# Mamba layers in a four-layer kernel: the residual by TensorE, the softplus correction by ScalarE and GpSimd, the norm's affine part in the weights

## The chip, the cores and the metric

The kernel runs on one core of a Trainium2 chip. A core has five instruction streams: TensorE (PE, matrix products into PSUM), VectorE (DVE), ScalarE (ACT), GpSimd (POOL) and SyncE (SP), which here issues all DMA transfers. The streams run side by side and wait for each other by semaphores; each works through its own list in order. The metric is the time of one execution on the device in microseconds (us). Everything is float32.

## The reference

The input has 4 images of 96 channels and 64 x 64 points. Four layers follow each other: a Mamba layer, a state-space layer over four scan directions, a second Mamba layer and a ConvNeXt block. The change concerns the two Mamba layers only. Each treats an image as a sequence of L = 4096 tokens and runs two sublayers, then a 1x1 fusion and a batch norm. A sublayer is, cut to what matters:

```python
h = (seq - mu) * rsqrt(var + EPS) * ln_g + ln_b
xs, z = split(h @ in_w)                               # 192 + 192 channels
xc = silu(conv_b + sum(conv_w[:, k] * xp[:, k:k+L] for k in range(4)))   # xp: xs padded by 3
dt, Bm, Cm = split(xc @ xproj_w)                      # 6 + 16 + 16
delta = softplus(dt @ dt_w + dt_b)
# for each channel d and state s of 16, along the sequence:
#   state = exp(delta * A) * state + delta * Bm * xc
y = sum over s of state * Cm + Dp * xc
seq = seq + (y * silu(z)) @ out_w
```

The softplus of x is max(x, 0) + ln(1 + u), with u = exp(-|x|). Since u is small here and 1 + u is rounded, the kernel adds a correction: what was lost in the rounding, u - ((1 + u) - 1).

## The kernel before

One function, `mamba_fusion`, runs a Mamba layer. All four images stay in the tile `X` (96 channels on the partitions). Work goes in 32 steps: 2 pairs of images, times 2 sublayers, times 8 chunks of 512 tokens. A step has two parts.

The *front* (`mamba_front`, a generator) turns a chunk of both images of a pair into what the scans need. It normalises (`pc` and `pv` are matmuls for the centred values and the variance, L172 and L179; DVE multiplies, L184; POOL applies `ln_g` and `ln_b`, L185) into the tile `h`. A row of ones below the 96 channels serves for the convolution's bias. The convolution and the input projection are one set of matmuls, `pu` (L194), as are those for z, `pz` (L204). `pd` (L217) gives dt, B and C; `rows` and `bc` carry B and C through DRAM, to be spread over partitions. Then come three tiles of softplus (`pt` L235, function `softplus` L260 to L271), `du` = delta times xc (L248, POOL), and the stores of delta and du to DRAM (`dd` and `dg`, L251).

The *scan* (class `Scan`) treats a step as 24 groups of 2 x 512 columns on 128 partitions (8 channels by 16 states). A group needs exp(delta A) and delta B x. `load` brings delta from DRAM, spread over the states (`da`, L295); ACT takes the exponential (L107). For 18 of 24 groups the second term is a matmul that spreads `du` (`bs`, L313), multiplied by B on DVE (L335); for the other six ("dma" in the code) it is loaded and multiplied on POOL (L308). DVE runs two scans a group (`hs`, L340), POOL multiplies by C (`hc`, L342), and PE sums over the states (`py`, L361). After eight groups `close` (L369) multiplies by the gate, and for each image `project` (L377, into `po`) and a DVE addition to `X` (L381) end the sublayer. After the second sublayer, `fuse` applies the 1x1 fusion (`pf`, L510), takes the statistics (`bn_stats`, L512) and stores `X` to DRAM (`raw`, L513).

`Scan.run` writes the order. A slot is one group; stages run at a lag to it: loads 4 slots ahead, `spread` one ahead, `sums` two behind, `close` three, `project` four, `fuse` five behind. In each slot it also advances the front of the next step, as many pieces as the list `PACE` says:

```python
for lag, what in ((4, self.project), (5, self.fuse)):
    if (g := at(lag)) and g["last"] and g["j"] and (g["sub"] or lag == 4):
        what(g, g["j"] - 1)
for _ in range(PACE[slot] if slot < len(PACE) else 0):
    next(ahead, None)
```

The pieces with the softplus fall in the last slots of a step, beside the scans of groups 16 to 23 of the step before (counting groups from 0 in their step). From this program a scheduler derives the final order of each engine, and moves an instruction by some places. Buffers matter too: `bs` has two PSUM tiles[...], the front's matmuls share two banks under the tag `mm`, `py` and `po` (with `pf`) have one each; `hs` and `hc` have three buffers, `da` and `du` loads share six.

Of the kernel before, what the change touches and what calls it, by code (L numbers as in the profile page):

```python
# [18 lines left out]
F32 = mybir.dt.float32  # L19
AF = mybir.ActivationFunctionType  # L20
ALU = mybir.AluOpType
# [55 lines left out]
class Consts:  # L77
    def __init__(self, tc, pool):
        nc = tc.nc
        self.act = Tables(tc)  # L80
        self.norms = [pool.tile([C, 2], F32, name=f"bn{i}") for i in range(2)]
        self.ident = pool.tile([P, P], F32, name="ident")
        make_identity(nc, self.ident)

        self.center = pool.tile([C, C], F32, name="center")
        nc.vector.tensor_scalar(self.center, self.ident[:C, :C], -1.0 / C, None, ALU.add)
        self.mean = pool.tile([C, C], F32, name="mean")
        nc.vector.memset(self.mean, 1.0 / C)
        self.eps = pool.tile([P, 1], F32, name="eps")
        nc.vector.memset(self.eps, EPS)  # L90


class Tables:
# [61 lines left out]
def mamba_front(tc, k, X, pools, wt, pair, c, h, made):  # L155

    nc = tc.nc  # L160
    work, psum, dram = pools
    if c == 0:
        nc.vector.memset(h[:C, :, 0:3], 0.0)
    else:
        nc.scalar.copy(h[:C, :, 0:3], h[:C, :, T : T + 3])

    def bank(name):
        return psum.tile([P, T], F32, tag="mm", name=name)

    for b in range(2):  # L170
        pc = bank("pc")[:C]
        nc.tensor.matmul(  # L172
            pc, lhsT=k.center, rhs=X[:, 2 * pair + b, ds(c * T, T)], start=True, stop=True
        )
        sq = work.tile([P, T], F32, tag="ua", name="sq")[:C]
        nc.scalar.activation(sq, pc, AF.Square)
        yield
        pv = bank("pv")[:C]
        nc.tensor.matmul(pv, lhsT=k.mean, rhs=sq, start=True, stop=True)  # L179
        rs = work.tile([P, T], F32, tag="lg", name="rs")[:C]  # L180
        rsqrt(k.act, rs, pv, k.eps[:C])
        yield
        dst = h[:C, b, 3 : 3 + T]
        nc.vector.tensor_tensor(dst, pc, rs, ALU.mult)  # L184
        nc.gpsimd.tensor_scalar(dst, dst, wt["ln"][:, 0:1], wt["ln"][:, 1:2], ALU.mult, ALU.add)  # L185


    xz = made["xz"] = work.tile([P, 6, T], F32, name="xz", bufs=2)
    for j in range(3):
        pu = bank("pu")  # L190
        for tap in range(4):
            kk = C + 1 if tap == 3 else C
            for r0, r1, d0, d1, b in SEGS[j]:
                nc.tensor.matmul(  # L194
                    pu[r0:r1], lhsT=wt["conv"][:kk, tap, d0:d1], rhs=h[:kk, b, ds(tap, T)],
                    start=(tap == 0), stop=(tap == 3),
                )
            yield
        nc.scalar.copy(xz[:, j], pu)
    k.act.other(xz[:, :3], xz[:, :3], AF.Silu)  # L200
    for j in range(3):
        pz = bank("pz")
        for r0, r1, d0, d1, b in SEGS[j]:
            nc.tensor.matmul(  # L204
                pz[r0:r1], lhsT=wt["in"][:, DIN + d0 : DIN + d1], rhs=h[:C, b, 3 : 3 + T],
                start=True, stop=True,
            )
        yield
        nc.scalar.copy(xz[:, 3 + j], pz)


    dbl = work.tile([P, T], F32, name="dbl")
    pd = bank("pd")
    for n in range(2):
        for b in range(2):
            j, r0, r1 = ROWS[b][n if b == 0 else 1 - n]
            nc.tensor.matmul(  # L217
                pd[2 * QUART * b : 2 * QUART * (b + 1)], lhsT=wt["xproj"][r0:r1, j],
                rhs=xz[r0:r1, j], start=(n == 0), stop=(n == 1),
            )  # L220
    yield
    nc.scalar.activation(dbl, pd, AF.Identity, bias=wt["one"])


    rows = dram.tile([P, T], F32, name="rows")
    nc.sync.dma_start(rows, dbl)
    bc = made["bc"] = work.tile([P, 2, 2, T], F32, name="bc", bufs=2)


    du = made["du"] = work.tile([P, 3, T], F32, name="du", bufs=2)  # L230
    for j in range(3):
        pt = bank("pt")
        for r0, r1, d0, d1, b in SEGS[j]:
            half = ds(HALFP * b, HALFP)
            nc.tensor.matmul(  # L235
                pt[r0:r1], lhsT=wt["dt"][half, d0:d1], rhs=dbl[half], start=True, stop=True,
            )
        delta = work.tile([P, T], F32, name="delta", bufs=2)
        softplus(nc, k.act, work, delta, pt)
        yield  # L240
        if j == 0:
            for b in range(2):
                for q in range(2):
                    r = HALFP * b + (QUART if q else RANK + 1)
                    nc.sync.dma_start(
                        bc[:, b, q], rows[r : r + NST, None].to_broadcast([NST, HEIGHT, T])
                    )
        nc.gpsimd.tensor_tensor(du[:, j], delta, xz[:, j], ALU.mult)  # L248
        for name, x in (("dd", delta), ("dg", du[:, j])):
            made[name, j] = dram.tile([P, T], F32, name=f"{name}{j}")  # L250
            nc.sync.dma_start(made[name, j], x)  # L251
    k.act.other(xz[:, 3:], xz[:, 3:], AF.Silu)

PACE = (1,) * 8 + (2,) + (1,) * 7 + (2,) + (1,) * 7
LEAD = 4


def softplus(nc, act, work, out, x):  # L260

    u = work.tile([P, T], F32, tag="ua", name="ua")
    t = work.tile([P, T], F32, tag="lg", name="lg")
    nc.scalar.activation(u, x, AF.Abs)
    act.exp_ln(u, u, AF.Exp, scale=-1.0)
    act.exp_ln(t, u, AF.Ln, bias=1.0)
    nc.vector.scalar_tensor_tensor(out, x, 0.0, t, ALU.max, ALU.add)
    nc.scalar.activation(x, u, AF.Identity, bias=1.0)

    nc.vector.scalar_tensor_tensor(t, x, 1.0, u, ALU.subtract, ALU.subtract, reverse1=True)  # L270
    nc.gpsimd.tensor_tensor(out, out, t, ALU.add)  # L271


class Scan:
# [7 lines left out]


    def __init__(self, tc, k, X, pools, sel, carry, fuse):
        self.tc, self.k, self.X, self.sel, self.carry, self.fuse = tc, k, X, sel, carry, fuse
        self.state, self.psum = pools

    def load(self, g):
# [82 lines left out]
    def project(self, g, b):  # L371

        nc = self.tc.nc
        xz, wt = g["made"]["xz"], g["wt"]
        po = self.psum.tile([P, T], F32, tag="po", name="po", bufs=1)[:C]
        for n, (j, r0, r1) in enumerate(ROWS[b]):
            nc.tensor.matmul(  # L377
                po, lhsT=wt["out"][r0:r1, j], rhs=xz[r0:r1, j], start=(n == 0), stop=(n == 1)
            )
        xs = self.X[:, 2 * g["pair"] + b, ds(g["c"] * T, T)]  # L380
        nc.vector.tensor_tensor(xs, xs, po, ALU.add)  # L381

    def run(self, steps, wts, front, first):

# [9 lines left out]
        ]  # L394
        total, each = len(groups), len(units)
        ahead = iter(())
        for n in range(-4, total + 6):
            slot = (n + LEAD) % each
            if slot == 0:
                for _ in ahead:  # L400
# [4 lines left out]
            def at(lag):  # L405
                return groups[n - lag] if 0 <= n - lag < total else None
# [6 lines left out]
                if g := at(lag):  # L413
                    stage(g)

            for lag, what in ((4, self.project), (5, self.fuse)):
                if (g := at(lag)) and g["last"] and g["j"] and (g["sub"] or lag == 4):
                    what(g, g["j"] - 1)
            for _ in range(PACE[slot] if slot < len(PACE) else 0):
                next(ahead, None)  # L420


def mamba_weights(nc, act, ident, wpool, w, sub, one7):
    wt = {"one": one7}

    def load(name, shape):
        wt[name] = wpool.tile(shape, F32, name=f"w_{name}{sub}")
        nc.sync.dma_start(wt[name], w[name][sub])

    load("ln", [C, 2])  # L430
    load("in", [C, 2 * DIN])
    conv = wt["conv"] = wpool.tile([C + 1, 4, DIN], F32, name=f"w_conv{sub}")
    nc.sync.dma_start(conv[:C], w["conv_wT"][sub].partition_broadcast(C))
    nc.sync.dma_start(conv[C : C + 1, 3], w["conv_b"][sub : sub + 1])
    nc.vector.tensor_tensor(
        conv[:C], conv[:C], wt["in"][:, None, :DIN].to_broadcast([C, 4, DIN]), ALU.mult
    )
    xp = wt["xproj"] = wpool.tile([P, 3, 2 * QUART], F32, name=f"w_xproj{sub}")
    nc.vector.memset(xp, 0.0)
    nb = RANK + 1 + NST  # L440
# [26 lines left out]
def mamba_fusion(ctx: ExitStack, tc, k, src, dst, w):  # L467
# [38 lines left out]
    def fuse(g, b):  # L506
# [2 lines left out]
        pf = psum.tile([P, T], F32, tag="po", name="pf", bufs=1)[:C]  # L509
        nc.tensor.matmul(pf, lhsT=fus[:, 0], rhs=xs, start=True, stop=True)  # L510
        nc.scalar.activation(xs, pf, AF.Identity, bias=gb[:, b : b + 1])
        nc.vector.bn_stats(stats[:, b * NT + c], xs)  # L512
        nc.sync.dma_start(dst[b, :, ds(c * T, T)], xs)  # L513

    wts = [mamba_weights(nc, k.act, k.ident, one, w, 0, one7)]
    carry = one.tile([P, 3, P // HEIGHT], F32, name="carry")
    steps = [(pair, sub, c) for pair in range(B // 2) for sub in range(2) for c in range(NT)]

# [10 lines left out]
    for n, _ in enumerate(front(0, made)):  # L529
        if n % 4 == 3 and n // 4 - 1 in range(B):  # L530
            b = n // 4 - 1
            nc.vector.reduce_sum(gsum[:, b : b + 1], X[:, b], axis=AX.X)
    wts.append(mamba_weights(nc, k.act, k.ident, one, w, 1, one7))

    gpw = one.tile([C, C], F32, name="gpw")
    nc.sync.dma_start(gpw, w["gp_wT"])
# [12 lines left out]
    gb = one.tile([C, B], F32, name="gb")  # L549
    nc.scalar.activation(gb, pg2, AF.Identity, bias=vec[:, 1:2])  # L550

    Scan(tc, k, X, (state, psum), sel, carry, fuse).run(steps, wts, front, made)

    norm = k.norms.pop()
    mv = one.tile([C, 2], F32, name="mv")
# [733 lines left out]
```

## Time and profile before

| | |
|---|---|
| runs of the kernel before | 10000.75, 10018.09, 10055.14 us (median 10018.09) |
| profiled execution, its own time | 10010.64 us |
| its span, first to last instruction | 10008.9 us |
| busy, share of the span | PE 86%, DVE 82%, POOL 70%, ACT 55% |
| granted TensorE clock, mean | 0.939 of full speed |

"Busy" counts an engine's instructions, not its waits. The shares are means over four layers with different limits, so the stages are read apart. In a row of instruction groups, `L342 POOL TENSOR_TENSOR hc<-hs,bc 128x1024 x391` is line 342 on POOL, writing `hc` from `hs` and `bc` on 128 partitions by 1024 elements, 391 times; then busy time, the mean duration in ns, the engine's idle time just before these instructions, and what ended it. A float32 matmul counts as two instructions.

### The profile page before, as it was taken

To read this page: it belongs to the slowest core of one execution; us is meant where nothing else is said; L and a number is where in the kernel's file an instruction comes from. 1 tells how busy PE (TensorE), PEld (TensorE's weight loads), DVE (VectorE), ACT (ScalarE), POOL (GpSimd) and SP (SyncE) were. 2 spreads that over 40 slices of the span, in tenths; PEclk is the share of its full clock that TensorE was granted. 3 is DMA by queue.
4 is the path that set the end of the run, shared out by engine and by line. 5 is a ranking of instruction groups with operands and counts; after the bars stand their busy time and mean duration, and the time that the engine had idled before them with its cause. 6 is when DMAs were issued, how large, how long until landed. Compare 5 with 4: busy or idle time off the path is not lost. (4 is left out here: it accounts for less than half of the span.)

```text
span 10008.9 us, 110272 instructions
## 1 busy us (share of the span) xinstructions
PE 8562.4 (86%) x33120; PEld 3566.0 (36%) x33120; DVE 8200.6 (82%) x10877; ACT 5497.9 (55%) x10460; POOL 6966.5 (70%) x4600
## 2 busy tenths in 40 slices
PE   7888888888886888888888888788888888887688
PEld 1222212222214766666776676122222222221122
DVE  7999999999994666667666666799999999999787
ACT  5566666656653445445445444566666665665244
POOL 6888888888883555555555555688888888888322
PEclk9999999999997999999999999899999999999798
DMA  7777777777773223223222221777777767777442
GB/s 190 200 205 204 201 206 207 201 201 209 204 197 105 72 66 94 65 66 95 72 66 74 81 64 51 188 201 204 210 200 203 208 196 204 207 204 199 113 99 73
DMA packets 802257, 1527.53 MB, mean 153 GB/s; under 512 B 123933, under 2 KB 127161, under 8 KB 800890
## 3 DMA queue, kind: packets, MB, share of 16 engines
q1 hardware_dynamic: 801658, 1520.47, 54.6%
q8 instruction: 263, 4.31, 0.2%
q14 instruction: 336, 2.75, 0.1%
HBM read 1229.30 MB, written 155.98 MB: 138 GB/s over the span
## 5 line engine op out<-in xcount | busy, mean ns | idle before, releaser
L342 POOL TENSOR_TENSOR hc<-hs,bc 128x1024 f32<-128x1024 f32 x1536 | 3608.0, 2355 | 622.2 <-DVE hs L340 554.8
L340 DVE TENSOR_TENSOR_SCAN hs<-da,carry,bs 128x512 f32<-128x512 f32 x2016 | 2466.4, 1264 | 79.2 <-POOL du L308 1.0
L107 ACT ACTIVATE da<-da,w_a 128x512 f32<-128x512 f32 x2304 | 1616.5, 716 | 1268.5 <-DMA da<-dd 1218.7
L361 PE MATMUL py<-hc,selsum 128*32 128x512 f32 x6144 | 1801.4, 638 | 462.5 <-POOL hc L342 448.3
L313 PE MATMUL bs<-du,seldu 64*128 64x512 f32 x4608 | 1573.3, 676 | 204.2 <-DVE hs L340 194.5
L335 DVE TENSOR_TENSOR bs<-bs,bc 128x1024 f32<-128x1024 f32 x1152 | 1397.7, 1213 | 184.0 <-PE bs L313 181.6
L308 POOL TENSOR_TENSOR du<-du,bc 128x1024 f32<-128x1024 f32 x384 | 904.5, 2355 | 281.3 <-DMA du<-dg 160.5
L863 POOL TENSOR_TENSOR seg<-seg,cb 128x384 f32<-128x384 f32 x512 | 514.7, 1006 | 818.1 <-DVE cb L862 750.0
L361 PEld LDWEIGHTS py<-hc,selsum 128*32 128x32 f32 x6144 | 240.6, 110 | 1815.1 <-POOL hc L342 1118.2
L313 PEld LDWEIGHTS bs<-du,seldu 64*128 64x128 f32 x4608 | 446.0, 195 | 1196.2 <-DVE hs L340 852.1
L848 DVE TENSOR_SCALAR seg<-dr,dac 128x128 f32<-128x128 f32 x1536 | 660.4, 458 | 256.9 <-PE y L892 249.3
L194 PE MATMUL pu<-h,w_conv 96*128 96x512 f32 (+3 forms) x2048 | 834.6, 629 | 6.5 <-ACT rs L107 6.3
L340 DVE TENSOR_TENSOR_SCAN hs<-bs,carry,du 128x512 f32<-128x512 f32 x672 | 823.5, 1260 | 7.8 <-issue 5.0
L799 PE MATMUL front<-pk,sconv 128*128 128x512 f32 x1536 | 767.9, 609 | 9.2 <-ACT z L787 5.1
L915 ACT ACTIVATE y<-yz 128x192 f32<-128x192 f32 x512 | 186.0, 363 | 919.3 <-DVE yz L914 918.3
L867 POOL TENSOR_TENSOR xs<-pre,coef 128x576 f32<-128x576 f32 x512 | 598.3, 1175 | 56.2 <-ACT pre L112 31.5
L810 PE MATMUL front<-sconv,pk 128*128 128x192 f32 x3072 | 577.2, 330 | 45.3 <-DVE pre L815 36.0
L1152 DVE SCALAR_TENSOR_TENSOR acc<-pad,c_conv,acc 96x1024 f32<-96x1024 f32 x336 | 491.9, 1468 | 109.1 <-ACT acc L1143 58.0
L902 POOL TENSOR_TENSOR y<-y,xs 128x192 f32<-128x192 f32 x496 | 293.5, 592 | 412.8 <-DVE y L901 412.1
L345 ACT COPY carry<-hs 128x2 f32<-128x2 f32 x1344 | 250.7, 187 | 564.2 <-DVE hs L340 560.4
L107 ACT ACTIVATE bs<-da,w_a 128x512 f32<-128x512 f32 x768 | 522.0, 680 | 2.5 <-DMA da<-dd 0.7
L810 PEld LDWEIGHTS front<-sconv,pk 128*128 128x128 f32 x3072 | 497.4, 191 | 69.3 <-DVE pre L815 57.7
(191 smaller groups left out, 13881.2 us busy)
## 6 DMA issues: line engine op xcount, KB each, us to landing
da<-dd SPq DMA_DIRECT2D x3072, 256.0 KB
du<-dg SPq DMA_DIRECT2D x768, 256.0 KB
dr<-rows SPq DMA_DIRECT2D x256, 384.0 KB
bc<-rows SPq DMA_DIRECT2D x256, 256.0 KB
dd<-delta SPq DMA_DIRECT2D x192, 256.0 KB
dg<-du SPq DMA_DIRECT2D x192, 256.0 KB
pk<-xn SPq DMA_DIRECT2D x128, 384.0 KB
pk<-xn SPq DMA_DIRECT2D x128, 256.0 KB
```

The source lines that it names most:

```text
L107: self.last = self.scalar.activation(out, in_, func, **kw)
L194: nc.tensor.matmul(pu[r0:r1], lhsT=wt["conv"][:kk, tap, d0:d1], rhs=h[:kk, b, ds(tap, T)], start=(tap == 0), stop=(tap == 3),)
L308: nc.gpsimd.tensor_tensor(g["du"], g["du"], self.b_or_c(g, 0), ALU.mult)
L313: nc.tensor.matmul(g["bs"][:, i], lhsT=self.sel["du"][rows, g["half"], g["q"]], rhs=g["made"]["du"][rows, g["j"]], start=True, stop=True,)
L335: nc.vector.tensor_tensor(dbx, dbx, self.b_or_c(g, 0), ALU.mult)
L340: nc.vector.tensor_tensor_scan(hs[:, i], da[:, i], dbx[:, i], init, ALU.mult, ALU.add)
L342: nc.gpsimd.tensor_tensor(g["hc"], hs, self.b_or_c(g, 1), ALU.mult)
L361: nc.tensor.matmul(py[rows], lhsT=self.sel["sum"][:, g["q"]], rhs=g["hc"][:, i], start=(g["q"] == 0), stop=(g["q"] == NQU - 1),)
L799: nc.tensor.matmul(p, lhsT=self.conv[:, i, DI + q * DST : DI + (q + 1) * DST], rhs=pk[:, i, ds(c * T, T)], start=(i == 0), stop=(i == 2),)
L810: nc.tensor.matmul(p, lhsT=pk[:, i, ds(c * Q, Q)], rhs=self.conv[:, i, :DI], start=(i == 0), stop=(i == 2),)
L848: nc.vector.tensor_scalar(seg[:, h], g["pair"]["dr"][:, c % 2 * NH + h], made["dac"][:, n0 + h : n0 + h + 1], 0.0, ALU.subtract, ALU.min,)
L867: nc.gpsimd.tensor_tensor(xs, x.to_broadcast([P, 3, NH, HD]), coef.to_broadcast([P, 3, NH, HD]), ALU.mult)
```

## The change

Three things change inside a Mamba step, and their order with them.

The residual: `project` starts the accumulation in `po` with an identity matmul of the chunk of `X`, and a new stage `keep` copies the sum back to `X` on ACT. The stages after `project` (lag 4) are now `keep` (5), `fuse` (6) and `store` (7: statistics and the store to DRAM).

The softplus: 1 + u was written by ACT to PSUM and the correction formed by one DVE instruction, added by one on POOL. Now ACT forms 1 + u and then (1 + u) - 1 in SBUF in two Identity instructions, and POOL subtracts and adds. The three tiles go through three stages, one slot apart: (1) matmul, Abs, Exp, Ln; (2) max-and-add on DVE, the two Identities on ACT; (3) the three POOL instructions and the stores. That is four pieces of the generator for the former three, and two buffers each for the scratch tiles `ua` and `lg`.

The norm: `ln_g` is multiplied into the weights, and `ln_b` times the weights becomes a 97th row of them, against the row of ones in `h`. L185 is gone, and every matmul of `pu` and `pz` takes 97 rows. `mamba_weights` forms these weights with three more matmuls, copies and a scaling.

```diff
@@ mamba_front
-        nc.vector.tensor_tensor(dst, pc, rs, ALU.mult)
-        nc.gpsimd.tensor_scalar(dst, dst, wt["ln"][:, 0:1], wt["ln"][:, 1:2], ALU.mult, ALU.add)
+        nc.vector.tensor_tensor(h[:C, b, 3 : 3 + T], pc, rs, ALU.mult)
...
-                    pu[r0:r1], lhsT=wt["conv"][:kk, tap, d0:d1], rhs=h[:kk, b, ds(tap, T)],
+                    pu[r0:r1], lhsT=wt["conv"][:, tap, d0:d1], rhs=h[:, b, ds(tap, T)],
...
-                pz[r0:r1], lhsT=wt["in"][:, DIN + d0 : DIN + d1], rhs=h[:C, b, 3 : 3 + T],
+                pz[r0:r1], lhsT=wt["z"][:, d0:d1], rhs=h[:, b, 3 : 3 + T],
...
-    for j in range(3):
-        pt = bank("pt")
...
-        delta = work.tile([P, T], F32, name="delta", bufs=2)
-        softplus(nc, k.act, work, delta, pt)
-        yield
...
+    tiles = {}
+    for n in range(5):
+        if n >= 2:
+            j = n - 2
+            u, t, delta = tiles.pop(j)
+            nc.gpsimd.tensor_tensor(u, u, t, ALU.subtract)
+            nc.gpsimd.tensor_tensor(delta, delta, u, ALU.add)
+            nc.gpsimd.tensor_tensor(du[:, j], delta, xz[:, j], ALU.mult)
+            for name, x in (("dd", delta), ("dg", du[:, j])):
+                made[name, j] = dram.tile([P, T], F32, name=f"{name}{j}")
+                nc.sync.dma_start(made[name, j], x)
+        if n in range(1, 4):
+            u, t, pt = tiles[n - 1]
+            delta = tiles[n - 1][2] = work.tile([P, T], F32, name="delta", bufs=2)
+            nc.vector.scalar_tensor_tensor(delta, pt, 0.0, t, ALU.max, ALU.add)
+            nc.scalar.activation(t, u, AF.Identity, bias=1.0)
+            nc.scalar.activation(t, t, AF.Identity, bias=k.minus)
...
+        if n < 3:
+            pt = bank("pt")
...
+            u = work.tile([P, T], F32, tag="ua", name="ua", bufs=2)
+            t = work.tile([P, T], F32, tag="lg", name="lg", bufs=2)
+            nc.scalar.activation(u, pt, AF.Abs)
+            k.act.exp_ln(u, u, AF.Exp, scale=-1.0)
+            k.act.exp_ln(t, u, AF.Ln, bias=1.0)
+            tiles[n] = [u, t, pt]
+        if n < 4:
+            yield
-def softplus(nc, act, work, out, x):
...
-    nc.vector.scalar_tensor_tensor(out, x, 0.0, t, ALU.max, ALU.add)
-    nc.scalar.activation(x, u, AF.Identity, bias=1.0)
-    nc.vector.scalar_tensor_tensor(t, x, 1.0, u, ALU.subtract, ALU.subtract, reverse1=True)
-    nc.gpsimd.tensor_tensor(out, out, t, ALU.add)
@@ Scan.project
+        nc.tensor.matmul(po, lhsT=self.k.ident[:C, :C], rhs=xs, start=True, stop=False)
...
-        nc.vector.tensor_tensor(xs, xs, po, ALU.add)
+    def keep(self, g, b):
+        self.tc.nc.scalar.copy(self.X[:, 2 * g["pair"] + b, ds(g["c"] * T, T)], self.po)
@@ Scan.run
-            for lag, what in ((4, self.project), (5, self.fuse)):
+            for lag, what in ((4, self.project), (5, self.keep), (6, self.fuse), (7, self.store)):
@@ mamba_weights
+    both = wpool.tile([C + 1, 5, DIN], F32, name=f"w_conv{sub}")
+    conv, z = wt["conv"], wt["z"] = both[:, :4], both[:, 4]
...
+    for n in range(0, 5, 2):
+        m = min(2, 5 - n)
+        ps = psum.tile([P, T], F32, tag="mm", name="ps")[: C + 1, : m * DIN]
+        nc.tensor.matmul(ps, lhsT=shift, rhs=both[:C, n : n + m], start=True, stop=True)
+        nc.scalar.copy(both[C:, n : n + m].rearrange("p k n -> p (k n)"), ps[C:])
+    nc.vector.tensor_tensor(conv[C:, 3], conv[C:, 3], wx[C:], ALU.add)
+    nc.vector.tensor_scalar_mul(both[:C], both[:C], wt["ln"][:, 0:1])
```

## The prediction, made before the changed kernel had run

> **What bounds the kernel now.** I first read the busy time by stretches (columns: window, its length, then busy us and count on PE, PEld, DVE, ACT, POOL, then clock, DMA share, GB/s).
>
> ```profile
> 1000.00:2000.00 1000.00, 876.76 (x2700) 203.39 (x2698) 937.45 (x868) 626.07 (x1125) 853.66 (x409) 0.96 0.73 204
> 3300.00:6100.00 2800.00, 2452.87 (x13657) 1940.97 (x13656) 1871.65 (x4768) 1370.09 (x3157) 1515.84 (x1841) 0.96 0.26 74
> ```
>
> The first line is Mamba, the second the middle block, which the change leaves alone. Mamba fills about 0 to 3050 and 6350 to 9300: 64 steps of 24 groups. Between 1000 and 2500 L369 runs 49 times, three a step: 1500 x 3 / 49 = 91.8 us a step. DVE is busy 94% of it, but PE 88% and POOL 85%, so two others stand close behind the first. Next, what DVE waits for in 1000 to 2500 (total, times, longest):
>
> ```profile
> DVE bs L335 <- PE bs L313: 45.3, 37, 2.3
> DVE lg L270 <- ACT pt L268: 10.5, 16, 2.0
> DVE h L184 <- ACT rs L107: 8.2, 10, 1.4
> ```
>
> It is some 6% idle, half of that for PE's `bs`. Then the durations (busy, mean ns | idle before):
>
> ```profile
> L342 POOL TENSOR_TENSOR hc<-hs,bc 128x1024 f32<-128x1024 f32 x391 | 918.6, 2356 | 139.7 <-DVE hs L340 122.2 <-PE py L361 12.3 <-PE pv L179 2.7
> L271 POOL TENSOR_TENSOR delta<-delta,lg 128x512 f32<-128x512 f32 x48 | 60.8, 1266 | 0.1
> L270 DVE SCALAR_TENSOR_TENSOR lg<-pt,ua 128x512 f32<-128x512 f32 x48 | 32.6, 679 | 11.5 <-ACT pt L268 10.5 <-POOL du L308 0.9
> L381 DVE TENSOR_TENSOR X<-X,po 96x512 f32<-96x512 f32 x33 | 22.0, 666 | 0.7 <-PE bs L313 0.7
> L185 POOL TENSOR_SCALAR h<-h,w_ln 96x512 f32<-96x512 f32 x34 | 26.1, 768 | 0.0
> ```
>
> Last, POOL in order of time in one step, where the softplus falls among groups 16 to 23 (start, us):
>
> ```profile
> 1159.95 2.35 POOL L342 TENSOR_TENSOR hc<-hs,bc 128x1024 f32<-128x1024 f32 x1 [1.71 <-DVE hs L340]
> 1162.27 1.26 POOL L271 TENSOR_TENSOR delta<-delta,lg 128x512 f32<-128x512 f32 x1
> 1163.60 1.26 POOL L248 TENSOR_TENSOR du<-delta,xz 128x512 f32<-128x512 f32 x1
> 1164.94 4.71 POOL L342 TENSOR_TENSOR hc<-hs,bc 128x1024 f32<-128x1024 f32 x2
> 1169.77 2.35 POOL L308 TENSOR_TENSOR du<-du,bc 128x1024 f32<-128x1024 f32 x1
> 1172.08 2.35 POOL L342 TENSOR_TENSOR hc<-hs,bc 128x1024 f32<-128x1024 f32 x1
> 1174.53 1.27 POOL L271 TENSOR_TENSOR delta<-delta,lg 128x512 f32<-128x512 f32 x1
> 1175.88 1.26 POOL L248 TENSOR_TENSOR du<-delta,xz 128x512 f32<-128x512 f32 x1
> 1178.29 2.35 POOL L342 TENSOR_TENSOR hc<-hs,bc 128x1024 f32<-128x1024 f32 x1 [1.15 <-DVE hs L340]
> ```
>
> POOL runs back to back from `hc` 16 (1159.95) and only catches DVE again at `hc` 20 (1178.29): here it has no room left, though over a step it is 15% idle.
>
> **The skill.** GPSIMD Engine Reference, 3.1, prices a float32 `tensor_tensor` add of 2048 elements at 4497 ns, so I estimate 1124 ns for 512; the trace has 1266, which I use. Its 4.1 says that GpSimd has no path to PSUM: in the trace no POOL group reads a PSUM tile, and the softplus must first bring 1+u to SBUF. TensorE: Matmul & The Clock Gate, "Step-by-step", says that matmuls stay in program order and only weight loads are pulled ahead. The trace agrees: PE loses 102.1 us in 1000 to 2500 at `py` (L361) waiting for POOL's `hc`, with other matmuls queued behind.
>
> **The change, part by part, for a step.**
>
> DVE loses three L270 and two L381. Its records overlap by about 0.05 us, so the starts show 0.6 us each: 3.0 us. With L270 goes its wait (11.5 us over 16 steps, 0.7). Unhindered, DVE needs 3.7 us less.
>
> POOL gains three subtractions at 1.27 and loses two L185 at 0.77: +2.3 us, from 78.5 to about 80.8. That fits in a step; the place does not. In the changed order of POOL, from `hc` 16 on, stand: hc16, subtract, add, hc17, multiply, subtract, add, multiply, L308's `du` product, hc18, hc19, subtract, add, multiply, hc20. That is the pattern of nearly every step: all nine softplus operations come ahead of hc20, where four do now. By the starts above, a 1024-wide product takes 2.33 us and a dependent 512-wide one 1.33. After: 6 x 2.33 + 9 x 1.33 = 26.0 us from the end of scan 16 to the end of hc20; before: 6 x 2.33 + 4 x 1.33 = 19.3. DVE alone would end scan 20 after about 15.5 us, so POOL falls some 8 us, two groups, behind.
>
> Who waits: PE, in order, has half of `py` 20, then `pf` (second sublayer only), `pv`, then `bs` 23, which DVE's product 23 needs. These take 0.5 + 1.05 + 1.05 + 1.1 = 3.7 us, 2.65 without `pf`. The landing of the second `du` load, issued behind a store that waits for POOL, I put at 0.5 (bounds 0 and 2: other loads here land 3 to 5 us after issue). So product 23 starts 26.0 + 0.5 + 3.7 = 30.2 us after scan 16 (29.2 in the first sublayer). Before, it started at 26.1 (1159.70 to 1185.81), and 24.4 in a first-sublayer step at 510.80. From there to the third close DVE has 1.1 + 0.6 + 2.4 + 1.3 + 2.4 + 0.6 + 2.4 = 10.8 us. So 41.0 and 40.0 us after, against 37.5 and 37.1 in those steps before: +3.5 and +2.9, mean +3.2. This already counts the DVE instructions saved there, three L270 and one L381.
>
> PE gains two identity matmuls, about 1.05 us each (`pc`, of the same form, takes 1.10 in the timeline). One projection now has a matmul between two `bs`, ahead of `pz` and `pd`, where DVE already waits 1.8 us (at 1151.89): +1.05. The other falls where PE has about 1.2 us to spare; +0.2. The other L381 gone: -0.6. Together +0.65.
>
> ACT gains three Identities at 0.59 and two copies at 0.58, +2.9 us on 57.5: hidden, being 63% busy, and its Identities end before POOL reaches the subtractions. Uncovered they would cost those 2.9 us. L185 leaves the path to `pu` (0.8 us each, cover for PE only). Queued on SP, the stores of the first two tiles now wait for POOL just ahead of the loads of groups 22 and 23; these are needed 7 us later, so nothing. One column more in the weights' matmuls costs PE nothing visible: 96 and 97 rows took 1.12 and 1.13. The fusing step and its store come one and two groups later; the next user of their bank is eight groups away, so nothing. Weight preparation adds three matmuls, three copies and two small DVE operations, four times, mostly beside the first loads of X: between -4 and +15 us in all, taken as +5.
>
> Sum: 62 steps have a next one's front, 62 x 3.2 = 198; 64 x 0.65 = 42; 5. Together +245. The profiled execution took 10010.6 us (span 10008.9), 7 below the median, 10018: I predict 10256.
>
> **Rivals.** *DVE's gain comes through* (17%): DVE is the busiest engine, and 3.7 x 64 = 237 us give about 9775. Against it: POOL's 26 us are counted from the order and the durations. It wins, on the other side of zero, if POOL's excess costs DVE under 3.7 us a step, that is if hc20 trails scan 20 by less than about two groups' time (7.3 us), which are the slack between `hc` and `py`.
>
> *The two cancel* (11%): part of the 8 us is regained, since PE's `bs` waits that are now 2.8 us a step vanish in the new rhythm; 9970 to 10120, about 10050.
>
> *Loads come late too* (15%): SP stands still until the second tile's multiply, loads 21 to 23 land after ACT wants them, and ACT, in order, holds back the terms of group 21. For it: ACT has waited 5.1 us for one such load, at 1172.45. Two to three us more a step: 10430.
>
> The main case has 57%.
>
> **How the numbers follow.** The main case's own range is 10150 to 10360 (1.7 us a step either way). From 9960 to 10400 leaves out most of the first rival and the end of the third, under 2 in 10. Half a per cent (50 us) is about what this kernel's runs can tell (10000.8 to 10055.1). Slower: 57 + 15 + a part of the cancelling case, 0.74; same 0.09; faster 0.17.
>
> **What would show it.** Right: POOL's `hc` stops waiting for DVE between groups 17 and 21; DVE's wait for PE's `bs` rises from 2.8 to some 7 us a step; PE's wait for `hc` at `py` grows; steps of 95 to 96 us; L270 and its wait gone. Wrong: a step of 88 to 90 us with DVE at 94% or more, or DVE waits for `da` by ACT or DMA, or for `hs` buffers held by POOL, in place of `bs`.

## The result, and the profile after

The changed kernel takes 10475.46 us (10460.81 to 10477.99), the kernel before 10015.12 beside it: a ratio of 1.045, 95% interval 1.0418 to 1.0481. It is slower by 460 us; the prediction said slower, by 245, and its range ended at 10400. The profiled execution has a span of 10473.2 us, a mean granted clock of 0.905 (before 0.939), and DVE busy 77% of it (before 82%). DVE did less and waited more.

The busy time of the Mamba stretch from 1000 to 2000 us, after (columns as in the prediction: length, then busy us and count on PE, PEld, DVE, ACT, POOL, then clock, DMA share, GB/s):

```profile
1000.00:2000.00 1000.00, 848.08 (x2469) 192.03 (x2468) 829.00 (x743) 579.61 (x1061) 799.73 (x385) 0.90 0.69 187
```

No engine is above 85% now. DVE falls from 937 to 829, and nothing else rises in its place. What it waits for, 1000 to 2500 (total, times, longest):

```profile
DVE bs L340 <- PE bs L318: 144.4, 79, 6.8
DVE stats L539 <- ACT X L534: 36.3, 14, 3.3
DVE delta L245 <- POOL du L237: 19.1, 12, 1.7
```

The wait for PE's `bs` was 45.3; the other two are new. The rows of POOL and PE after, that answer to those of before (busy, mean ns | idle before):

```profile
L347 POOL TENSOR_TENSOR hc<-hs,bc 128x1024 f32<-128x1024 f32 x359 | 842.7, 2355 | 206.0 <-DVE hs L345 184.2 <-PE py L366 16.0 <-PE bs L318 2.3
L366 PE MATMUL py<-hc,selsum 128*32 128x512 f32 x1428 | 442.9, 666 | 154.5 <-POOL hc L347 152.2 <-DVE xz L374 0.6
L236 POOL TENSOR_TENSOR delta<-delta,ua 128x512 f32<-128x512 f32 x45 | 57.1, 1269 | 3.4
```

Single operations of POOL and DVE last what they did before; PE's `py` takes 666 ns on average (630 in the same window before). POOL's `hc` waits more for DVE (184 against 122 us), PE's `py` more for `hc` (152 against 102), DVE more for `bs`: three engines wait for each other in turn. POOL in order of time, in a step of the first sublayer (scan 16 ends at 543.45):

```profile
543.70 2.35 POOL L347 TENSOR_TENSOR hc<-hs,bc 128x1024 f32<-128x1024 f32 x1 [1.72 <-PE pt L259]
546.01 1.27 POOL L235 TENSOR_TENSOR ua<-ua,lg 128x512 f32<-128x512 f32 x1
547.36 1.28 POOL L236 TENSOR_TENSOR delta<-delta,ua 128x512 f32<-128x512 f32 x1
...
565.69 1.26 POOL L237 TENSOR_TENSOR du<-delta,xz 128x512 f32<-128x512 f32 x1
566.91 6.95 POOL L347 TENSOR_TENSOR hc<-hs,bc 128x1024 f32<-128x1024 f32 x3
```

From `hc` 16 to the first of the three at 566.91, which is `hc` 20 and ends at 569.2, POOL has no gap: 25.5 us from the start of `hc` 16, 25.7 from the end of scan 16, where the prediction had 26.0. PE and DVE at the end of this stretch:

```profile
563.10 1.92 PE L366 MATMUL py<-hc,selsum 128*32 128x512 f32 x4 [0.40 <-POOL hc L347]
564.95 2.08 PE L318 MATMUL bs<-du,seldu 64*128 64x512 f32 x4
569.31 1.91 PE L366 MATMUL py<-hc,selsum 128*32 128x512 f32 x2 [2.28 <-POOL hc L347]
571.15 1.89 PE L181 MATMUL pv<-sq,mean 96*96 96x512 f32 x2
572.97 1.13 PE L318 MATMUL bs<-du,seldu 64*128 64x512 f32 x4
574.15 1.23 DVE L340 TENSOR_TENSOR bs<-bs,bc 128x1024 f32<-128x1024 f32 x1 [3.29 <-PE bs L318]
```

PE waits for `hc` 20, runs half of `py` 20, then `pv`, then `bs` 23, and DVE has stood 3.29 us for it. That is the chain of the prediction, in its order. But `py`, `pv` and the first `bs` take 1.9 to 2.1 us where the same forms otherwise take 1.05 to 1.13: PE runs at half speed in these bursts (the granted clock is 0.5 from 552.30 to 572.78).

To see where a step grows, I cut it at the scans of the six groups loaded by DMA (1, 5, 9, 13, 17, 21), by the start of the first of the two scans of a group. Means over the first Mamba layer, us (steps run from scan 13 to the next step's scan 13; the last step of each pass of eight is left out):

| from scan to scan | 13-17 | 17-21 | 21-1 | 1-5 | 5-9 | 9-13 | step |
|---|---|---|---|---|---|---|---|
| before, first sublayer | 18.7 | 14.4 | 16.6 | 15.3 | 13.5 | 13.9 | 92.2 |
| before, second sublayer | 18.5 | 14.8 | 17.9 | 14.7 | 14.3 | 13.8 | 93.9 |
| after, first sublayer | 16.5 | 18.8 | 20.6 | 14.1 | 13.8 | 13.9 | 97.8 |
| after, second sublayer | 16.8 | 18.9 | 21.2 | 14.2 | 16.6 | 14.5 | 102.2 |

All steps of the layer together: 92.7 before, 99.8 after. The two profiles differ by 464 us. From the first scan of a layer to its last, the two layers take 445 us longer, 7.0 a step; 18 of the rest lie ahead of the scans, 5.8 before the first layer and 11.9 between the layers, stretches that hold the weights' preparation. Most lies between scans 17 and 1, where POOL is late. The second sublayer has 2.3 us more between scans 5 and 9, where the prediction had nothing.

### The profile page after: what moved, and what is told of

The parts are those of the page before. It is cut to its first block, busy times and chain, and to the rows that moved or that the text cites. A ratio compares the mean times of both kernels' runs of the same rounds, so it can differ in the third digit from the quotient of the medians.

```text
span 10473.2 us, 110596 instructions
## 1 busy us (share of the span) xinstructions
PE 8896.5 (85%) x33400; PEld 3615.0 (35%) x33400; DVE 8038.0 (77%) x10574; ACT 5576.9 (53%) x10730; POOL 7112.4 (68%) x4664
## 5 line engine op out<-in xcount | busy, mean ns | idle before, releaser
L366 PE MATMUL py<-hc,selsum 128*32 128x512 f32 x6144 | 1885.0, 663 | 678.9 <-POOL hc L347 669.5
L318 PE MATMUL bs<-du,seldu 64*128 64x512 f32 x4608 | 1509.8, 707 | 191.1 <-DVE hs L345 182.4
L193 PE MATMUL pu<-h,w_conv 97*64 97x512 f32 (+1 forms) x2048 | 838.6, 630 | 5.9 <-ACT rs L109 5.9
L345 DVE TENSOR_TENSOR_SCAN hs<-bs,carry,du 128x512 f32<-128x512 f32 x672 | 819.2, 1260 | 27.9 <-POOL hc L347 11.9
L318 PEld LDWEIGHTS bs<-du,seldu 64*128 64x128 f32 x4608 | 412.9, 202 | 1217.9 <-DVE hs L345 719.4
```

Source lines behind the costliest of these rows:

```text
L193: nc.tensor.matmul(pu[r0:r1], lhsT=wt["conv"][:, tap, d0:d1], rhs=h[:, b, ds(tap, T)], start=(tap == 0), stop=(tap == 3),)
L318: nc.tensor.matmul(g["bs"][:, i], lhsT=self.sel["du"][rows, g["half"], g["q"]], rhs=g["made"]["du"][rows, g["j"]], start=True, stop=True,)
L345: nc.vector.tensor_tensor_scan(hs[:, i], da[:, i], dbx[:, i], init, ALU.mult, ALU.add)
L366: nc.tensor.matmul(py[rows], lhsT=self.sel["sum"][:, g["q"]], rhs=g["hc"][:, i], start=(g["q"] == 0), stop=(g["q"] == NQU - 1),)
```

## The experiments

Each was timed beside the kernel before, which took 10017 to 10034 us (medians) in these series. Times are medians, with the ratio to it and the interval.

**1. The softplus back as it was.** In the changed kernel, `mamba_front` has the loop of before, with one piece a tile, and the function `softplus`:

```diff
-    tiles = {}
-    for n in range(5):
...
+    for j in range(3):
+        pt = bank("pt")
...
+        delta = work.tile([P, T], F32, name="delta", bufs=2)
+        softplus(nc, k.act, work, delta, pt)
+        yield
```

> The changed kernel with the softplus of before (one correction on DVE, one addition on POOL); residual by TensorE and norm in the weights stay. POOL-queue theory (nine softplus operations ahead of the product of group 20 hold back PE and then DVE): the burst is as short as before, most of the loss goes, 9980 to 10150, granted clock back near 0.93. Rival, PE's two identity matmuls and the later statistics are the cause: the loss stays, above 10300.

10239.94 us, 1.0216 (1.0193 to 1.0239). It missed both values. Some 236 us of the loss go with the softplus; 214 us over the kernel before stay in the residual and the norm, for which the prediction had 47.

**2. The residual back as it was.**

```diff
-        nc.tensor.matmul(po, lhsT=self.k.ident[:C, :C], rhs=xs, start=True, stop=False)
...
+        nc.vector.tensor_tensor(xs, xs, po, ALU.add)
-   ((4, self.project), (5, self.keep), (6, self.fuse), (7, self.store))
+   ((4, self.project), (5, self.fuse))
```

> The changed kernel with the residual of before (addition on DVE, statistics right after the fusion's copy); softplus in stages and norm in the weights stay. POOL-queue theory: the nine operations still precede the product of group 20, so still slow, 10200 to 10400. Rival, PE's identity matmuls or ACT's copies are the cause: back to 10000 to 10100.

10250.78 us, 1.0222 (1.0205 to 1.024): as the theory said, though by its number alone this is only half the story. The other half, 225 us, is the residual's. POOL's chain is as long here (538.68 to 564.3 in the step that was read), but PE's order at its end differs:

```profile
558.17 1.92 PE L365 MATMUL py<-hc,selsum 128*32 128x512 f32 x4 [3.57 <-POOL hc L346]
560.02 2.08 PE L317 MATMUL bs<-du,seldu 64*128 64x512 f32 x4
562.03 1.19 PE L181 MATMUL pv<-sq,mean 96*96 96x512 f32 x2
563.15 1.13 PE L317 MATMUL bs<-du,seldu 64*128 64x512 f32 x4
564.40 1.05 PE L365 MATMUL py<-hc,selsum 128*32 128x512 f32 x4
```

The second `bs` here (group 23) comes ahead of the `py` that needs `hc` 20; in the changed kernel it comes behind it. So the residual, which touches neither, decides here whether DVE pays for POOL's lag once more. This holds for the first sublayer only, where the mean from scan 21 to 1 is 16.5 us in this run, against 20.6 in the changed kernel. In the second it is 20.8 against 21.2, and there half of `py` 20 stands ahead of `bs` 23 with the residual of before too (read at 1230.15).

**3. The correction left out.** POOL's subtraction and addition are gone, six of nine operations a step; ACT's two Identities stay:

```diff
-            nc.gpsimd.tensor_tensor(u, u, t, ALU.subtract)
-            nc.gpsimd.tensor_tensor(delta, delta, u, ALU.add)
```

> The changed kernel without POOL's subtraction and addition of the correction (six of the nine operations of a step; the correction is left out, all else stays). POOL-queue theory: 6 x 1.33 = 8 us of POOL's queue in the burst go, about what it lagged; DVE is back to its own pace but for the matmul ahead of pz and the statistics' wait: 64 steps of 89 to 91 us, 9850 to 9980. Rival, PE or ACT load or the statistics are the cause: above 10250.

9936.4 us, 0.9911 (0.9896 to 0.9925): as POOL's theory said. 539 us are 8.4 a step, and six operations at 1.33 are 8.0: in this stretch POOL's time is paid in full.

**4. The statistics without their wait**, from a tile `still` that is ready from the start; the kernel leaves out the statistics of `X`.

```diff
-        nc.vector.bn_stats(stats[:, b * NT + c], xs)
+        nc.vector.bn_stats(stats[:, b * NT + c], still)
```

> The changed kernel with the statistics taken of a constant tile, so that they wait for nothing and run at the start of a layer (the batch norm's scale is then not that of the reference). If DVE's wait for the fused chunk (36.3 us in 15 steps) adds to the time: 32 second-sublayer steps x (1.9 to 2.6 us + 1.2 us of the statistics themselves), less some 20 us at the start: 10340 to 10410. If it only stands in for the wait for bs that would follow: 10430 to 10480.

10477.04 us, 1.0448 (1.0431 to 1.0466): no change. The wait for the statistics is gone, and DVE waits longer for `bs` in its place (192.8 us in 1000 to 2500, against 144.4).

**5. Only the norm changed, in the kernel before.** The diff is the norm's part of the change: L185 gone, 97-row weights, `mamba_weights`.

> The kernel before with the norm's affine part in the weights, and nothing else of the change. With the softplus undone 214 us of the loss stayed, in the residual and the norm together; this run and the next split them. Theory, the residual holds all of it: POOL has two L185 less (1.5 us a step) and the order of PE is that of before, so 9930 to 10030. Rival, the 97-row weights or their preparation carry it: 10100 or more.

10051.65 us, 1.0036 (1.0026 to 1.0046). Neither: it costs 36 us by the ratio. In the profile, 43 us longer than that of before, the first Mamba layer's scans begin 1.5 us later and take 17 longer, the stretch between the layers takes 11 more, the second layer's scans 12 more. L185's 1.5 us of POOL a step brought nothing.

**6. Only the residual changed, in the kernel before.**

```diff
+        nc.tensor.matmul(po, lhsT=self.k.ident[:C, :C], rhs=xs, start=True, stop=False)
...
-        nc.vector.tensor_tensor(xs, xs, po, ALU.add)
+    def keep(self, g, b):
+        self.tc.nc.scalar.copy(self.X[:, 2 * g["pair"] + b, ds(g["c"] * T, T)], self.po)
-   ((4, self.project), (5, self.fuse))
+   ((4, self.project), (5, self.keep), (6, self.fuse), (7, self.store))
```

> The kernel before with the residual by TensorE, the copy back on ScalarE and the later fuse and store, and nothing else of the change. Theory, the residual holds the 214 us: 10200 to 10300, with DVE's waits for PE's bs near 6 to 7 us a step, and PE in the order po, bs, pt in place of bs, pt, po. Rival, the norm holds it: 10000 to 10060, since DVE has 1.2 us a step less to do and PE 2.1 more.

10216.57 us, 1.0196 (1.017 to 1.0223): 200 us, as the theory said. PE and DVE in a step of it:

```profile
525.94 1.09 PE L380 MATMUL po<-xz,w_out 64*96 64x512 f32 x2 [0.79 <-DVE xz L370]
527.78 1.05 PE L362 MATMUL py<-hc,selsum 128*32 128x512 f32 x2 [0.75 <-POOL hc L343]
528.76 1.13 PE L314 MATMUL bs<-du,seldu 64*128 64x512 f32 x4
529.93 1.23 DVE L336 TENSOR_TENSOR bs<-bs,bc 128x1024 f32<-128x1024 f32 x1 [3.20 <-PE bs L314]
```

The projection's last matmul, which waits for DVE's gate, and a `py`, which waits for `hc`, now stand ahead of `bs`. In the kernel before, `bs` came first, then `pt`, `py` and the projection:

```profile
510.93 1.13 PE L313 MATMUL bs<-du,seldu 64*128 64x512 f32 x4 [0.47 <-DVE hs L340]
514.43 1.12 PE L235 MATMUL pt<-dbl,w_dt 64*128 64x512 f32 x2
516.46 0.67 PE L377 MATMUL po<-xz,w_out 64*96 64x512 f32 x1
```

DVE's wait for `bs` in 1000 to 2500 is 104.9 us (before 45.3). By the cut of the table the cost lies between scans 13 and 17: 23.0 and 23.4 us in the two sublayers, against 18.7 and 18.5 before. Run 1, which keeps this residual, has 22.8 and 23.8 in the same place.

**7. The same without the identity matmuls**; the residual sum is left out.

```diff
-        nc.tensor.matmul(po, lhsT=self.k.ident[:C, :C], rhs=xs, start=True, stop=False)
```

> The run before this one without the identity matmuls: the residual sum is left out, X becomes the projection alone; copies on ScalarE, late fuse and late store stay. Its PE order is that of the kernel before again. Theory, the identity matmul and the order that it brings are the loss: 9930 to 10030. Rival, the copies or the late fuse and store are the loss: 10150 or more.

9985.68 us, 0.9968 (0.9953 to 0.9983): as the theory said. Copies and late stages are no loss in the kernel before.

**8. The subtractions on DVE, in the changed kernel.**

```diff
-            nc.gpsimd.tensor_tensor(u, u, t, ALU.subtract)
+            nc.vector.tensor_tensor(u, u, t, ALU.subtract)
```

> The changed kernel with the three subtractions of the correction on DVE in place of POOL. POOL then has the softplus operations of before (two 512-wide ones a tile, stages kept), DVE three small ones more, 3 x 0.6 us a step, +115 us if nothing hides them. Theory, POOL's queue in the softplus stretch is what costs: 3.9 us a step go, 10200 to 10350. Rival, the stages of one slot each cost, whoever does the arithmetic: 10450 or more.

10185.23 us, 1.0168 (1.0143 to 1.0193): 290 us less, though DVE has three operations a step more. A little better than the theory's range. DVE's wait for `bs` in 1000 to 2500 is 51.6 us, against 144.4.

**9. The residual alone, its identity matmul last in `po`.** 

```diff
-        nc.tensor.matmul(po, lhsT=self.k.ident[:C, :C], rhs=xs, start=True, stop=False)
         for n, (j, r0, r1) in enumerate(ROWS[b]):
...
+        nc.tensor.matmul(po, lhsT=self.k.ident[:C, :C], rhs=xs, start=False, stop=True)
```

> The kernel before with the residual by TensorE alone, as in the residual's own run (10216.6), but with the identity matmul as the last of the three into po. The same matmuls and copies are done; on PE, bs and pt now come ahead of the second projection again, as in the kernel before. Theory, the order that the leading identity brought is the loss: 9960 to 10080. Rival, the 2.1 us of identity matmuls a step are the loss themselves: 10150 to 10250.

10074.2 us, 1.0048 (1.0029 to 1.0067). The same work in another order costs 46 us over its own kernel before, where it had cost 200. On PE, `bs` (512.68) again comes ahead of `pt` (516.16) and the projection (518.19), as in the kernel before. There the identity matmul costs mostly by the order that the scheduler gives PE because of it.

**10. The changed kernel, its identity matmul last** (same edit).

> The changed kernel with the identity matmul last in po; all else as it is, POOL's nine softplus operations too. Theory, the two parts of the loss lie in different waits and add up: some 200 us go, 10230 to 10330. Rival, POOL's lag holds PE wherever the identity stands: 10420 or more.

10465.69 us, 1.0436 (1.0416 to 1.0456): the rival's value. The theory of two independent parts falls.

**11. Both mends, the subtractions on DVE and the identity last.**

> The changed kernel with both mends: the three subtractions on DVE, the identity matmul last. It computes all that the kernel before does. Theory, additive: 10185 less some 200, so 9950 to 10060. Rival, the mends overlap: 10120 or more.

10177.2 us, 1.0152 (1.0135 to 1.0168), the rival's value again: the second mend adds nothing.

**12. The kernel before without the correction.**

```diff
-    nc.scalar.activation(x, u, AF.Identity, bias=1.0)
-    nc.vector.scalar_tensor_tensor(t, x, 1.0, u, ALU.subtract, ALU.subtract, reverse1=True)
-    nc.gpsimd.tensor_tensor(out, out, t, ALU.add)
```

> The kernel before with the softplus's correction left out (ACT's 1 + u, DVE's L270, POOL's addition), nothing else. In the changed kernel the correction cost 539 us. DVE does 1.8 us a step less and loses L270's wait (0.7), POOL 3.8 less. Theory, before, its POOL part is hidden and DVE's is not: 9820 to 9900. Rival, PE and its waits bound the stretch already: 9980 to 10030.

10001.02 us, 0.9975 (0.9966 to 0.9983): the rival's value. All of the correction cost 27 us before; its POOL part alone cost 539 after the change. So the three L270 of a step, which the change set out to save, were almost free to begin with.

**13. The changed kernel without the identity matmuls** (the edit of 7); the residual sum is left out.

> The changed kernel without the identity matmuls: the residual sum is left out, X becomes the projection alone. Copies on ScalarE, late fuse and late store stay. Theory, the identity matmuls and PE's order with them are the residual's share: 10230 to 10300. Rival, the copies and the later stages are: 10420 or more.

10327.08 us, 1.0305 (1.0275 to 1.0334): between the two values. The matmuls and the order with them are 148 us of the residual's 225 here.

**14. The changed kernel, `po` copied back by DVE.**

```diff
-        self.tc.nc.scalar.copy(self.X[:, 2 * g["pair"] + b, ds(g["c"] * T, T)], self.po)
+        self.tc.nc.vector.tensor_copy(self.X[:, 2 * g["pair"] + b, ds(g["c"] * T, T)], self.po)
```

> The changed kernel with the copy of po back to X on DVE in place of ScalarE; the identity matmuls stay. DVE does 1.2 us a step more, 77 us if nothing hides it. Theory, PE's matmuls and order are the share: 10450 to 10560. Rival, the copies wait in ScalarE's queue and hold po and the statistics: 10300 or less.

10332.09 us, 1.0304 (1.0285 to 1.0324): 143 us less with more work for DVE. Neither number, but nearer the rival. 143 and the 148 of run 13 are more than the 225 of the residual together, so the two overlap. What ACT waits for at the fusion, 1000 to 2500, in the changed kernel:

```profile
ACT X L534 <- PE pf L533: 57.7, 7, 8.9
```

and with the copy on DVE:

```profile
ACT X L534 <- PE pf L533: 9.3, 6, 2.7
```

PE's order has changed with the copy, though: in the step that was read, `pf` (1136.70) stands ahead of `py` 20 (1141.07) here and behind it in the changed kernel. And ACT stands more for `pv`, 80.2 us against 65.3. So the 143 us are the copy's together with the order that came of it, and no price of ACT's wait alone.

**15. The subtractions on DVE and the residual of before**; only norm and stages are left of the change.

> The changed kernel with the subtractions on DVE and the residual of before; the norm in the weights and the stages stay, and it computes all that the kernel before does. Theory, POOL's subtractions and the residual are all of the loss, and the stages cost nothing: 9960 to 10060. Rival, the stages cost by themselves: 10130 or more.

10119.6 us, 1.0091 (1.0073 to 1.0109). Nearer the rival: beyond the norm's 36 us, the three stages with the subtraction on DVE cost some 57 us.

**16. The correction left out and the residual of before.**

> The changed kernel with the correction left out of the softplus, and the residual of before: 9936.4 was measured with the residual by TensorE. Theory, the residual's share comes on top whatever POOL does: 9720 to 9820. Rival, without POOL's lag the residual costs little: 9890 to 9950.

9855.63 us, 0.9829 (0.9806 to 0.9851): below the rival's range, above the theory's. Without POOL's lag the residual still costs 81 us. This is the fastest kernel measured, but it leaves the correction out; none that computes all was faster than the kernel before.

**17. Fusion and statistics three groups later, in the changed kernel.**

```diff
-   ((4, self.project), (5, self.keep), (6, self.fuse), (7, self.store))
+   ((4, self.project), (5, self.keep), (9, self.fuse), (10, self.store))
```

> The changed kernel with the fusion (fuse) at lag 9 and the statistics and store at lag 10, three groups later each; the order of everything else stays. Theory, ScalarE's stand at the fusion (8.2 us a step of the second sublayer) and pf ahead of bs 23 on PE cost some 3 us in each of 32 steps: 10340 to 10400, and second-sublayer steps near 99 us. Rival, these waits only stand in for the wait for bs, as the statistics did: 10440 or more.

10395.69 us, 1.0364 (1.0345 to 1.0382): the theory's value, 80 us less. Steps of the second sublayer fall from 102.2 to 99.5 us, nearly all of it between scans 5 and 9 (16.6 to 14.3), and those of the first stay. But the wait that the theory named is not what went. In the changed kernel ACT stands for `pf`, which stands on PE behind the `py` of `hc` 20; with the late fusion it stands as long in the same place for `pv`:

```profile
1269.28 0.68 ACT L534 ACTIVATE X<-pf,gb 96x512 f32<-96x512 f32 x1 [8.75 <-PE pf L533]
1269.71 0.69 ACT L109 ACTIVATE rs<-pv,numbers 96x512 f32<-96x512 f32 x1 [8.88 <-PE pv L181]
```

In 1000 to 2500 this wait for `pv` rises from 65.3 to 119.3 us, as that for `pf` falls from 57.7 to 1.2. What went is at the second image's fusion, after scan 5 of the next step. In the changed kernel:

```profile
1199.62 0.72 ACT L109 ACTIVATE da<-da,w_a 128x512 f32<-128x512 f32 x1 [5.00 <-DMA da<-dd]
1200.25 0.67 ACT L534 ACTIVATE X<-pf,gb 96x512 f32<-96x512 f32 x1
1200.95 0.69 DVE L539 BATCH_NORM_STATS2 stats<-X 96x6 f32<-96x512 f32 x1 [2.71 <-ACT X L534]
```

The copy of the fused chunk stands in ACT's queue behind an exponential that waits 5.00 us for its load, and DVE's statistics stand for the copy. It does not take POOL's lag: without the correction (run 3) scans 5 to 9 still take 16.7 us. And without the identity matmuls (run 13), where the copy does not stand behind such a wait, they take 14.3.

## Why the prediction was half right

*Direction and mechanism: right.* POOL becomes late in the softplus stretch (26.0 us forecast, 25.7 measured), PE waits in order, DVE waits for `bs`. Runs 3 and 8 show it: POOL's operations, taken away or moved, give back 539 and 290 us. The signs that it named are there: no gap of POOL between `hc` 16 and 20, `py`'s wait for `hc` up, L270 and its wait away. But a step takes 97.8 and 102.2 us, not 95 to 96, and DVE's wait for `bs` went not to 7 but to 144.4 / (1500 / 99.8) = 9.6 us a step. In place of L270's wait stands a new one, `delta`'s for POOL (19.1 us).

*The softplus's term: right in size, in part by luck.* It was 62 x 3.2 = 198 us. With the residual of before (run 2) the change costs 225, and the norm alone 36 of it, so 189 are left. The halves do not agree: the steps of run 2 grow by 1.6 us in the first sublayer and by 5.3 in the second, some half a microsecond of the norm included, where +2.9 and +3.5 were forecast. In the first, `bs` 23 came ahead of `py` 20, so the forecast chain does not hold there without the new residual.

*The stretch from scan 16 to the third close: the mechanism right, the size off.* Forecast were 40.0 and 41.0 us for the two sublayers. Over the first layer's steps (last of each pass left out, from the end of scan 16 to the start of the third close) it is 41.7 and 42.5 on average, against 36.6 and 37.4 before: +5.1 in both, where +2.9 and +3.5 were forecast. In the step shown, POOL is on time (25.7 us against 26.0), and the missing part is PE's: from the end of `hc` 20 to `bs` 23 it needs 3.7 us for half of `py` and `pv`, where the sum had 0.5 and 1.05. Half a `py` lasts as long as a whole one (1.05 us, at 574.03), and both ran at half the clock. The 0.5 put for the landing of a load did not show.

*The residual's term: the step that failed.* It was "+1.05 ... +0.2 ... -0.6. Together +0.65" a step, 42 us in all. It measured 200 us alone (run 6) and 225 in the changed kernel (run 2). I had counted the two identity matmuls by their durations and looked at the places where they stand. Runs 7 and 9 show what that left out in the kernel before: without them 31 us less than before, with them first 200 more, with the same work last 46 more. The matmul's own time is not what cost most; `bs` slid behind matmuls that wait for POOL and DVE (run 6). In the changed kernel its place no longer matters (run 10), but taking it out gives 148 us (run 13). The residual's cost lies elsewhere there: against run 2, from scan 21 to 1 in the first sublayer (20.6 us against 16.5) and from 5 to 9 in the second (16.6 against 14.4).

*"The fusing step and its store come one and two groups later ... so nothing": wrong.* I named the next user of the bank, and not what stands ahead in ACT's queue. Moving the fusion on gives back 80 us (run 17), between scans 5 and 9 of the second sublayer. The statistics' wait alone is not the price: without it those scans take 15.3 us in place of 16.6, and the time comes back as a wait for `bs` (run 4). How much is the copy's place on ACT and how much `pf`'s on PE was not split.

*DVE needs 3.7 us a step less: near, and worth nothing.* DVE's busy time on the whole falls from 8200.6 to 8038.0 us, 2.5 a step, where 3.0 of the 3.7 were instructions. Runs 7 and 12 would have told what that is worth before the change: in the kernel before, taking out the three L270 with the rest of the correction saves 27 us, and having the two additions to `X` off DVE, without the identity matmuls, 31. DVE was 94% busy, but PE and POOL were nearly as busy; that the removed ones stood where another engine was as close is argued and not tried.

*The norm: weights +5, else nothing.* 36 us measured. In the profile of run 5 29 of its 43 us lie in the steps, about half a microsecond each, whose cause was not tried, and 12 ahead of the layers' scans, where the weights are prepared and +5 had been put.

*The rival of late loads* had the nearest number, 10430, but not its waits: ACT waits for `da` by DMA 185.5 us in 1000 to 2000 after, 192.8 before. In 1000 to 2500 DVE never stands for `da`, and its wait for `hs` buffers is small (5.1 us). A small part of its mechanism is there, though: ACT, in order, does stand for a load and holds back the fusion's copy (run 17).

What stays open: how the residual's 225 us in the changed kernel split. Matmuls (148), the copy's place on ACT (143) and the fusion (80) overlap; without the matmuls, scans 21 to 1 stay long (21.9 and 21.6 us) and 17 to 21 and 5 to 9 get shorter. And what PE's half clock costs by itself was not tried.

## What to carry to other kernels

An engine that is 94% busy may still have no time to give: take the instructions out first, in a kernel that is allowed to leave them out, and see what they are worth. Price an addition to an in-order queue by what slides behind it, for every engine that it touches, and read the new order of that queue as one order: in the kernel before, the place of a matmul of 1 us decided whether `bs` stood ahead of or behind a `py` that waits for POOL (runs 6 and 9). And a wait can be a shadow: make the data early (run 4) before you believe that it costs. When a change does gain, look which wait went: in run 17 it was not the one that the theory had named.

## What the runs showed of the hardware

PE's clock falls where PE is busy for too small a part of a short window; it need not stand still for all of it. The granted clock in the traces has two values, 1 and 0.5, and changes only at whole multiples of 3.41 us. Two windows ahead of a fall, the first in the changed kernel, with the slow stretch after it, the last in run 6 (columns as in the prediction):

```profile
548.89:552.30 3.41, 1.30 (x5) 0.39 (x6) 1.71 (x3) 3.39 (x6) 3.41 (x3) 1.00 0.52 156
552.30:572.78 20.48, 14.70 (x24) 2.36 (x22) 13.85 (x12) 9.60 (x17) 20.17 (x12) 0.50 0.72 207
530.72:534.14 3.42, 2.29 (x5) 0.54 (x4) 3.42 (x5) 2.86 (x6) 2.23 (x2) 1.00 0.62 141
```

PE was busy 38% of the window in the first case and 67% in the second, where no wait in the 8 us before was as long as 1 us and the clock was 0.50 from 534.14 to 540.96. I cut the records of both kernels from 100 to 2500 us at these windows. At full clock, half clock followed 58 of 59 windows in which PE was busy under half of the time, 20 of 239 between 50 and 80%, and none of 908 above. From half clock, full clock followed none of 63 windows under 80% and 79 of 137 above. (PE's ends are modelled, so the shares are rough.)

The Trainium skill, TensorE: Matmul & The Clock Gate, "What's actually happening", says that the clock has two states, half and full, and falls to half after an idle window of about 3.4 us. The two states and the length of the window agree. The condition does not: 29 of the 31 falls before the change and 39 of the 47 after it came with no wait of PE as long as 3.41 us. The measurement decides. POOL's lag brings such windows: the mean granted clock between 100 and 2500 us is 0.96 before, 0.90 after, and 0.95 without the correction (run 3).
